# The second MLP's down projection as seven products of quarters, interleaved with the next unit's gate and up products

## The chip, the cores and the metric

The kernel runs on one core of one Trainium2 chip. The metric is device time in microseconds (us). A core has five engines that matter here: TensorE (PE, matrix products), VectorE (DVE), ScalarE (ACT), GpSimd (POOL) and SyncE (SP, which issues most DMAs). Each engine works through its own queue in order and waits on semaphores that other engines and DMAs raise. PE writes its products to PSUM, from which DVE and ACT read them. All data are float32, and 128 is the number of partitions (`P`).

## What is computed

Two layers are run on 2 sequences (`B`) of 1024 tokens (`T`), of 512 features (`D`), together 2048 tokens (`NT`). Each layer adds a product of two branches to its input:

```python
xn = _layernorm(x, axis=-1)
s = _L0_attn_ref(xn, ...)            # delta-rule attention, 16 heads of 128
g = _silu(_L0_ffn_ref(xn, ...))      # ternary MLP, 1408 wide
x = x + s * g
xn = _layernorm(x, axis=-1)
s = _L1_attn_ref(xn, ...)            # gated linear recurrence over the tokens
g = _silu(_L1_ffn_ref(xn, ...))      # the MLP that is changed here
x = x + s * g
```

The second MLP has 4096 hidden features. Its weights come packed as 4-bit codes with one scale for each block of 32:

```python
Wg = dequant_nvfp4(gate_W_packed, gate_scales)      # [4096, 512]
Wu = dequant_nvfp4(up_W_packed, up_scales)          # [4096, 512]
Wd = dequant_nvfp4(down_W_packed, down_scales)      # [512, 4096]
gate = jnp.einsum('th,nh->tn', xt, Wg)
up = jnp.einsum('th,nh->tn', xt, Wu)
gelu = jnp.tanh(0.7978845608028654 * (gate + 0.044715 * gate ** 3)) * gate * 0.5 + gate * 0.5
inter = gelu * up
out = jnp.einsum('tn,hn->th', inter, Wd)
```

The second layer's other branch forms, for each feature, two sigmoid gates by small block-diagonal products, and from them a recurrence h = a h + x over the 1024 tokens.

## The kernel before

**The order of the whole.** `first_layer` runs the attention and the ternary MLP. `Join.run` then goes over the 16 tiles of 128 tokens: `product` (L182) multiplies a tile of the attention's output by its weight (16 matmuls into `jpo`), and `rest` closes the layer for that tile: multiply by the MLP's branch (L199), add the input (L195, and a store of the new x to `x1d`), statistics (L190 to L192), POOL's power, and the normalisation. `turn` then transposes the tile twice (L113): once for the recurrence, copied by ACT and stored to `xd`, and once for the MLP, copied by DVE into quarters of `xq`. After each second tile four DVE subtractions form sums of quarters (t1, t2, t4 and b12). The last tile's `turn` is not called there: it is returned as `late` and called inside `second_layer`.

**Units of the MLP.** `second_layer` splits the 4096 hidden features into 16 groups (`NG`) of 256 and the tokens into the 2 sequences. The loop at the end runs over the groups `g` and, inside, the sequences `b`: one unit is one pair. A unit makes gate [256 x 1024], up [256 x 1024], their product, and the group's share of down, [1024 x 512].

**Gate and up.** Gate and up are matrix products by halves in all three directions, 2 x 2 x 2 blocks, and `four` (L1216 on) makes them by Strassen's scheme in Winograd's form: seven products of quarters in place of eight, with sums of quarters before and after. A `product` (L1229) is two matmuls of 512 columns, contracting 2 x 128 features, into one of four PSUM banks `psa` to `psd`. Banks a, c and d take a second product on top of the first, which adds without another engine. DVE does the other sums (L1239), ACT one copy (L1249), then ACT applies the gelu to the gate's four quarters (L1275), and DVE multiplies with up's quarters (L1281). The results `inter` are four tiles of 128 hidden features x 512 tokens.

**Down.** `down` goes over the unit's 8 tiles of 128 tokens. For each, two matmuls of 512 columns (L1306) contract the group's 2 x 128 hidden features into a bank of the pool `ps_o` (2 buffers), and DVE adds it to `acc`, one [128 x 512] sum for each of the 16 token tiles that stays in SBUF over all groups (L1317; a copy, L1315, in group 0). In the last group each tile is finished at once: SiLU on ACT (L1322), times the recurrence's output `y` on DVE, plus `x1` on POOL or DVE (L1325), and a store issued from ACT's queue.

**Weights.** `group_weights(g + 1)` is called ahead of the group's units. `unpack` loads codes and scales (SP) and turns them into float32 on DVE: five integer operations of 128 x 512, then one multiplication for each destination block (8 of 128 columns each for gate and for up, 2 of 512 for down). `quartered` adds four sums of quarters on POOL for gate and for up. Each of the three weights has two buffers in the pool `wp`; `qp` (2 buffers) holds the codes and scales.

**The recurrence beside.** `recur` handles one quarter of the features (`KC` = 4) of one sequence: block-diagonal products on PE (L1172), sigmoids, tanh and square root on ACT, reciprocals on DVE (L1187), multiplications on POOL (L1188), a scan on DVE, transposes on PE (L1205), a store to `yd`. It is a generator; one step is taken after most of the DVE additions of `four`. Before it, `softplus` (L90, L91 and on) prepares its constants from `vec`, on ACT and DVE.

**What sets the order.** In the second layer, the order on each engine is chosen by the scheduler of the framework from the dependencies and the program's order; nothing is pinned. `first_layer` has a local class `Ordered`, a thin wrapper around an engine that marks its instructions to stay in the order in which they are written while `order["loop"]` is set. Tiles come from pools: a tile takes the buffer of an older one of the same tag, and its first writer waits until that one's users are done. Pools that open after others have closed take over their room in SBUF, with the same kind of waits.

Of the kernel before, what the change touches and what calls it, by code (L numbers as in the profile page):

```python
# [103 lines left out]
def transposed(nc, psp, tag, dst, src, ident, engine, step=1):  # L104
# [11 lines left out]
    if engine == "scalar":  # L116
        nc.scalar.copy(dst, pt)
    else:
        nc.vector.tensor_copy(dst, pt)

# [131 lines left out]
def first_layer(ctx, tc, a, cst, minus_half, keep, xnT, od, gd, then):  # L252
# [247 lines left out]
    class Ordered:  # L500
        def __init__(self, engine):
            self.engine = engine

        def __getattr__(self, name):
            def call(*args, **kw):
                i = getattr(self.engine, name)(*args, **kw)  # L506
                if order["loop"]:
                    tc.keep_in_program_order(i)
                return i

            return call

    PE, DVE, ACT, POOL = (Ordered(e) for e in (nc.tensor, nc.vector, nc.scalar, nc.gpsimd))
# [560 lines left out]
def second_layer(ctx, tc, a, cst, x1d, xd, xq, out, late):  # L1074
# [11 lines left out]

    nc = tc.nc
# [4 lines left out]
    hp = ctx.enter_context(tc.tile_pool(name="l1_h", bufs=2, reuse_waits="tile"))  # L1092
# [4 lines left out]
    ident = cst[:, C_ID, :]  # L1097

# [3 lines left out]
    def unpack(name, src, scales, n, g):  # L1102

        pk = qp.tile([P, n], I32, tag="pk", name=f"pk_{name}_{g}")
        nc.sync.dma_start(pk, src)
        sc = qp.tile([P, n], F32, tag="sc", name=f"sc_{name}_{g}")
        nc.sync.dma_start(sc, scales)
        hi = qp.tile([P, n], I32, tag="hi", name=f"hi_{name}_{g}", bufs=1)
        nc.vector.tensor_scalar(hi, pk, 0xF0, 12, ALU.bitwise_and, ALU.logical_shift_left)
        nc.vector.scalar_tensor_tensor(  # L1110
            pk, in0=pk, scalar=0xF, in1=hi, op0=ALU.bitwise_and, op1=ALU.bitwise_or
        )
        nc.vector.tensor_scalar(hi, pk, 0x00070007, 9, ALU.bitwise_and, ALU.logical_shift_left)
        nc.vector.tensor_scalar(pk, pk, 0x00080008, 12, ALU.bitwise_and, ALU.logical_shift_left)
        nc.vector.tensor_tensor(pk, pk, hi, ALU.bitwise_or)
        halves = pk.bitcast(F16).rearrange("p (n par) -> p par n", par=2)

        def write(dst, par, at=slice(None)):
            nc.vector.scalar_tensor_tensor(
                dst, in0=halves[:, par, at], scalar=16384.0, in1=sc[:, at], op0=ALU.mult, op1=ALU.mult  # L1120
            )

        return write

    def quartered(name, g):

        write = unpack(name, a[name + "pk"][g], a[name + "sc"][g], 512, g)
        w = wp.tile([P, 7, 2, P], F32, tag=f"w_{name}", name=f"w_{name}_{g}")
        for par in range(2):
            for q in range(4):  # L1130
                write(w[:, q, par, :], par, slice(q * P, (q + 1) * P))
# [309 lines left out]
```

## Time and profile before

| | |
|---|---|
| median of 3 runs | 3302.39 us |
| lowest and highest | 3301.01 and 3304.95 us |
| profiled execution, its own time | 3295.65 us |
| its span in the trace | 3293.9 us |
| mean granted TensorE clock | 0.997 of full speed |
| instructions | 36429 |
| DMA traffic | 281.01 MB, 85 GB/s on average |

The page of the profile has the busy time of each engine, the span in 40 equal slices, the DMA queues, the chain of work that ended last, and the costliest groups of instructions. Lines such as "PE 98%" average over stages that differ: up to about 2014 us the first layer runs, with ACT and DVE mostly 30 to 80% busy and DMA at 75 GB/s or more in nearly all slices; behind it the second layer runs, with DMA mostly at 20 to 45 GB/s. PE's row of tenths is 9 or 8 in all slices after the first. One execution's span is 1.75 us shorter than the same execution's time, and that execution lies a little under the lowest of the three timed runs.

### The profile page before, as it was taken

Reading aid. Unit: us, or ns where it says so; the run is one execution under the profiler, and the core shown is the slowest. Engines: PE = TensorE matmul, PEld = TensorE weight load, DVE = VectorE, ACT = ScalarE, POOL = GpSimd, SP = SyncE. Lnnn points to the kernel's source line nnn. Section 1 sums busy time; section 2 is a strip of 40 time slices with the busy share of each in tenths; the row PEclk is TensorE's granted clock in tenths of the full one; section 3 lists DMA queues with packets and bytes.
Section 4 is the critical chain, followed back from the end, with each engine's and each line's share of the span. In section 5 each row is a group of like instructions: output and inputs, shape, how many; then the busy total and the mean of one; then the engine's idle time right before and its main releaser. Section 6 shows DMA issues by size and latency. Waiting matters only on the chain. (4 is left out here: it accounts for less than half of the span.)

```text
span 3293.9 us, 36429 instructions
## 1 busy us (share of the span) xinstructions
PE 3217.0 (98%) x11734; PEld 1807.1 (55%) x11734; DVE 2070.9 (63%) x4398; ACT 1138.5 (35%) x2093; POOL 619.6 (19%) x1008
## 2 busy tenths in 40 slices
PE   7999999999999999998999999999999999999998
PEld 6566756666666666665666444444444444444443
DVE  4566578686878777775664633676666655555545
ACT  3576455555465555444443001222222211100002
POOL 2000022322232222322322200122111100100002
PEclk9999999999999999999999999999999999999999
DMA  5244334444444444434324541111111100000003
GB/s 177 67 140 99 101 108 114 119 133 123 115 113 137 126 125 108 106 107 116 89 76 118 188 151 61 32 32 32 32 32 32 45 26 20 26 20 24 15 0 128
DMA packets 495039, 281.01 MB, mean 85 GB/s; under 512 B 206720, under 2 KB 438912, under 8 KB 494848
## 3 DMA queue, kind: packets, MB, share of 16 engines
q1 hardware_dynamic: 484544, 261.63, 28.2%
q0 software_dynamic: 5696, 8.65, 0.9%
q10 hardware_dynamic: 4608, 8.39, 0.7%
q8 instruction: 94, 1.54, 0.2%
q14 instruction: 97, 0.79, 0.1%
HBM read 179.71 MB, written 86.25 MB: 81 GB/s over the span
## 5 line engine op out<-in xcount | busy, mean ns | idle before, releaser
L1306 PE MATMUL po<-w_d,u 128*128 128x512 f32 x1024 | 455.2, 597 | 11.0 <-DVE acc L1317 5.4
L1306 PEld LDWEIGHTS po<-w_d,u 128*128 128x128 f32 x1024 | 189.3, 190 | 271.2 <-issue 206.1
L506 PE MATMUL pgate<-xnT,wg 128*128 128x512 f32 x512 | 249.4, 597 | 0.0
L1317 DVE TENSOR_TENSOR acc<-acc,po 128x512 f32<-128x512 f32 x240 | 162.9, 682 | 134.0 <-PE po L1306 133.0
L506 PE MATMUL pwv<-xnT,wv 128*128 128x512 f32 x512 | 245.0, 594 | 1.8 <-ACT gate L506 1.8
L506 PE MATMUL pwq<-xnT,wq 128*128 128x512 f32 x512 | 245.1, 593 | 0.0
L1249 ACT COPY g<-pga 128x512 f32<-128x512 f32 x32 | 18.7, 586 | 637.7 <-PE pga L1229 637.7
L506 PE MATMUL pwk<-xnT,wk 128*128 128x512 f32 x512 | 236.8, 593 | 1.6 <-ACT ka L506 1.6
L506 DVE SCALAR_TENSOR_TENSOR v<-prewv,cw,v 128x512 f32<-128x512 f32 x192 | 169.3, 883 | 64.6 <-ACT v L506 53.2
L182 PE MATMUL jpo<-wo,jo 128*128 128x512 f32 x416 | 181.0, 592 | 0.0
L506 DVE SCALAR_TENSOR_TENSOR ka<-prewk,cw,ka 128x512 f32<-128x512 f32 x192 | 146.8, 766 | 36.3 <-ACT ka L506 26.1
L506 DVE SCALAR_TENSOR_TENSOR q<-prewq,cw,q 128x512 f32<-128x512 f32 x192 | 160.3, 835 | 14.4 <-ACT q L506 8.0
L506 DVE TENSOR_TENSOR rr<-rr,zw 128x128 f32<-128x128 f32 x192 | 54.9, 286 | 175.1 <-PE zw L506 173.6
L506 PEld LDWEIGHTS zw<-rr,ground 128*128 128x128 f32 x512 | 96.1, 191 | 125.2 <-issue 98.2
L506 ACT COPY w<-zw 128x128 f32<-128x128 f32 x192 | 50.8, 265 | 328.8 <-PE zw L506 328.6
L1275 ACT ACTIVATE g<-g 128x512 f32<-128x512 f32 x96 | 60.4, 630 | 260.4 <-DVE g L1239 260.2
L506 PEld LDWEIGHTS zw<-w,ground 128*128 128x128 f32 x768 | 111.6, 192 | 66.4 <-issue 55.2
L506 POOL TENSOR_TENSOR rs<-rs,minus_half 128x4 f32<-128x4 f32 x64 | 64.5, 1007 | 421.8 <-DVE rs L506 397.9
L506 POOL TENSOR_TENSOR ot<-ot,gate 128x512 f32<-128x512 f32 x64 | 87.3, 1364 | 298.6 <-ACT ot L506 269.2
L506 ACT ACTIVATE on<-po,nm,rs 128x128 f32<-128x128 f32 x256 | 103.6, 460 | 90.0 <-DVE nm L506 90.0
L506 PEld LDWEIGHTS pwk<-xnT,wk 128*128 128x128 f32 x512 | 90.4, 190 | 76.9 <-issue 72.9
L182 PEld LDWEIGHTS jpo<-wo,jo 128*128 128x128 f32 x416 | 78.0, 190 | 92.3 <-issue 92.3
(248 smaller groups left out, 6520.4 us busy)
## 6 DMA issues: line engine op xcount, KB each, us to landing
e<-gr SPq DMA_DIRECT2D x64, 256.0 KB, 4.0
de<-e SPq DMA_DIRECT2D x64, 256.0 KB, 2.8
dk<-ka SPq DMA_DIRECT2D x32, 512.0 KB, 2.8
kb<-dk SPq DMA_DIRECT2D x64, 256.0 KB, 3.4
eb<-de SPq DMA_DIRECT2D x64, 256.0 KB, 3.0
eg<-egr SPq DMA_DIRECT2D x64, 256.0 KB, 3.9
od<-ot SPq DMA_DIRECT2D x64, 256.0 KB, 2.1
jo<-od SPq DMA_DIRECT2D x16, 1024.0 KB, 6.4
```

The lines of the kernel that those rows point to most:

```text
L182: matmul(po, lhsT=ot[:, h, :], rhs=self.wo[h], start=(h == 0), stop=(h == H - 1))
L506: i = getattr(self.engine, name)(*args, **kw)
L1249: nc.scalar.copy(c21, banks["a"])
L1275: nc.scalar.activation(ge[key], x, AF.Gelu_apprx_tanh)
L1306: nc.tensor.matmul(po, lhsT=inter[par, h][:, i * P : (i + 1) * P], rhs=wd[:, par, :], start=(par == 0), stop=(par == 1),)
L1317: nc.vector.tensor_tensor(dst, dst, po, ALU.add)
```

## The change

**Down by seven products.** For groups 0 to 14, `down` makes the unit's share by the same scheme as gate and up: tokens, hidden features and output features are each halved. Each of the seven products of quarters is made in two steps, one for each half of its 512 tokens. A step (`yield` in `down`) is two matmuls of 256 columns into one bank of `ps_o`, and one DVE addition of 128 x 512 to the accumulator of that product. So `acc` becomes two tiles of seven sums, one set for each sequence, which run over the groups, and the sums after the seven products are made once, by `together`: 28 DVE additions in the last two units. The sums of quarters before are new work in each group: of the weights, four on POOL in `halved`; of the intermediate result, four on POOL in `times`. Group 15 keeps the old form, two matmuls of 512 columns a tile, in `down_last`, which adds to the combined sums.

**Slots.** Down no longer stands behind its own unit. The main loop runs the 14 gate and up products of a unit as 14 slots, and each slot takes one step of the unit before's down, one step of the unpacking for the next group, and, in most slots, one step of the recurrence. The seventh product of up is made in the second slot of the next unit. Group 15's first eight tiles are finished in slots of the last unit, and the other eight behind it.

**Written order.** `Ordered` moves to module level, and the second layer's PE, DVE, ACT and POOL instructions go through it from the start of the main loop: each engine runs them in the order in which they are written. The unpacking of group 0 comes before that.

**Smaller parts.** `four` makes its first, second, fourth and seventh products in bank a (which has two buffers now, and where each of them adds to the one before), the third and sixth in c and the fifth in b; ACT copies bank a out after the first, the second and the fourth. `unpack` is a generator, its last multiplications write several blocks at once (two of 512 columns a weight in place of eight of 128), and its POOL sums run at the end. `recur` runs by halves of 512 tokens, 16 in all, with the state carried over in `carry`, one started in each of 16 units. The last loads of `y` and `x1` use buffers of `qp` and `rp`. The stores of the output are issued from SP's queue, in two halves of a row, and SiLU of a tile is written ahead of the finishing of the tile before.

```diff
...
+class Ordered:
+    def __init__(self, tc, engine, on):
+        self.tc, self.engine, self.on = tc, engine, on
+    def __getattr__(self, name):
+        def call(*args, **kw):
+            i = getattr(self.engine, name)(*args, **kw)
+            if self.on():
+                self.tc.keep_in_program_order(i)
+            return i
+        return call
...
-    hp = ctx.enter_context(tc.tile_pool(name="l1_h", bufs=2, reuse_waits="tile"))
+    hp = ctx.enter_context(tc.tile_pool(name="l1_h", bufs=1, reuse_waits="tile"))
...
+    order = {"on": False}
+    PE, DVE, ACT, POOL = (
+        Ordered(tc, e, lambda: order["on"]) for e in (nc.tensor, nc.vector, nc.scalar, nc.gpsimd)
+    )
...
         halves = pk.bitcast(F16).rearrange("p (n par) -> p par n", par=2)
-        def write(dst, par, at=slice(None)):
-            nc.vector.scalar_tensor_tensor(
-                dst, in0=halves[:, par, at], scalar=16384.0, in1=sc[:, at], op0=ALU.mult, op1=ALU.mult
+        for par in range(2):
+            to = dst(par)
+            k = to.shape[1]
+            DVE.scalar_tensor_tensor(
+                to,
+                in0=halves[:, par, :].rearrange("p (k n) -> p k n", k=k),
+                scalar=16384.0,
+                in1=sc.rearrange("p (k n) -> p k n", k=k),
+                op0=ALU.mult,
+                op1=ALU.mult,
             )
-        return write
+            yield
+        for s in sums:
+            POOL.tensor_tensor(*s)
...
+    def halved(g):
+        w = wp.tile([P, 7, 256], F32, tag="w_d", name=f"w_d_{g}")
+        b11, b12, b21, b22, t1, t2, t4 = (w[:, q] for q in range(7))
+        sums = (
+            (t1, b12, b11, ALU.subtract),
+            (t2, b22, t1, ALU.subtract),
+            (b12, b22, b12, ALU.subtract),
+            (t4, b21, t2, ALU.subtract),
+        )
+        return w, unpack("d", g, lambda par: w[:, 2 * par : 2 * par + 2], sums if g < NG - 1 else ())
...
+    weights, steps = group_weights(0)
+    done(steps)
...
+        def first():
+            product("a", A11, B11, True)
+            ACT.copy(p1, banks["a"])
+        def second():
+            product("a", S2, T2, False)
+            ACT.copy(u1, banks["a"])
+        def third():
+            product("c", S1, T1, True)
+        def fourth():
+            product("a", S3, T3, False)
+            ACT.copy(u2, banks["a"])
+            DVE.tensor_tensor(u2, u2, banks["c"], ALU.add)
+            last((1, 1), u2)
+        def fifth():
+            product("b", A12, B21, True)
+            add(p1, "b", (0, 0))
+        def sixth():
+            product("c", S4, B22, False)
+            add(u1, "c", (0, 1))
+        def seventh():
+            product("a", A22, T4, False)
+            last((1, 0), banks["a"])
+        return first, second, third, fourth, fifth, sixth, seventh
...
+            if key == (0, 1) and g == NG - 1:
+                inters[g, b] = [ups[0, 0], None, ups[0, 1], ups[1, 1]]
+            elif key == (0, 1):
+                s1, s2, s4 = (tile_of(t, u) for t in ("s1", "s2", "s4"))
+                a11, a21, a22 = ups[0, 0], ups[0, 1], ups[1, 1]
+                POOL.tensor_tensor(s1, a21, a22, ALU.add)
+                POOL.tensor_tensor(a21, a11, a21, ALU.subtract)
+                POOL.tensor_tensor(s2, s1, a11, ALU.subtract)
+                inters[g, b] = [a11, None, a21, a22, s1, s2, s4]
+            if key == (1, 0):
+                inters[g, b][A12] = x = ups[key]
+                if g < NG - 1:
+                    POOL.tensor_tensor(inters[g, b][S4], x, inters[g, b][S2], ALU.subtract)
...
+    def down(g, b, wd):
+        left = inters[g, b]
+        for i, j, n in (
+            (A22, T4, 3), (A11, B11, 0), (A12, B21, 1), (S3, T3, 6), (S1, T1, 4), (S2, T2, 5), (S4, B22, 2)
+        ):
+            for half in range(2):
+                po = ps_o.tile([P, 2, 256], F32, tag="pso", name=f"po_{g}_{b}_{n}_{half}")
+                for t in range(2):
+                    c = (2 * half + t) * P
+                    PE.matmul(
+                        po[:, t, :], lhsT=left[i][:, c : c + P], rhs=wd[:, j, :], start=True, stop=True
+                    )
+                dst = acc[b][:, n, half]
+                if g == 0:
+                    DVE.tensor_copy(dst, po)
+                else:
+                    DVE.tensor_tensor(dst, dst, po, ALU.add)
+                yield
...
+    def together(b):
+        P1, P2, P3, P4, P5, P6, P7 = range(7)
+        for dst, x, y in (
+            (P6, P1, P6), (P1, P1, P2), (P7, P6, P7), (P4, P7, P4), (P7, P7, P5), (P5, P6, P5), (P3, P5, P3)
+        ):
+            for half in range(2):
+                DVE.tensor_tensor(acc[b][:, dst, half], acc[b][:, x, half], acc[b][:, y, half], ALU.add)
+                yield
...
-                nc.scalar.activation(dst, dst, AF.Silu)
-                nc.vector.tensor_tensor(dst, dst, y, ALU.mult)
-                last = nc.gpsimd if b == 0 or h or i < 2 else nc.vector
-                last.tensor_tensor(dst, dst, x1, ALU.add)
-                nc.scalar.dma_start(out[ti * P : (ti + 1) * P, :], dst)
...
+    def last_steps(b, h, i, ti, dst):
+        y, x1 = (t.rearrange("p (h n) -> p h n", h=2) for t in at_last.pop(ti))
+        last = POOL if b == 0 or h or i < 2 else DVE
+        return (
+            lambda: DVE.tensor_tensor(dst, dst, y, ALU.mult),
+            lambda: last.tensor_tensor(dst, dst, x1, ALU.add),
+            lambda: nc.sync.dma_start(
+                out[ti * P : (ti + 1) * P, :].rearrange("t (h n) -> t h n", h=2), dst
+            ),
+            load_last,
+        )
...
+                dst = acc[b][:, 3:7:3, i // 2, i % 2] if h else acc[b][:, 0:3:2, i // 2, i % 2]
+                DVE.tensor_tensor(dst, dst, po, ALU.add)
+                ACT.activation(dst, dst, AF.Silu)
+                for step in finishing:
+                    step()
+                finishing = last_steps(b, h, i, ti, dst)
+                yield
+        for step in finishing:
+            step()
+        yield
...
+    order["on"] = True
+    before, recurring, downs, tog = None, none, none, none
+    steps = none
+    for n in range(2 * NG):
+        g, b = n // 2, n % 2
+        if b == 0:
+            wg, wu, wd = weights
+            done(steps)
+            if g < NG - 1:
+                weights, steps = group_weights(g + 1)
+        if n == 2 * NG - 2:
             for _ in range(4):
                 load_last()
-        for b in range(B):
-            inter = up_and_gate(g, b, wg, wu)
-            if g == 0 and b == 0:
-                late(ps_r, "psr", rp.tile([P, KC, P], F32, tag="y", name="xt_last"))
-            down(g, b, wd, inter)
+        if g == NG - 1:
+            tog = together(b)
+        lasts = none
+        if n == 2 * NG - 1:
+            lasts = down_last(0, wd)
+        for f, products in enumerate(up_and_gate(g, b, wg, wu)):
+            for s in range(7):
+                slot = 7 * f + s
+                if s == 1:
+                    if before:
+                        before()
+                else:
+                    products[s - (s > 0)]()
+                if n == 0 and slot == 3:
+                    late(ps_r, "psr", rp.tile([P, KC, P], F32, tag="y", name="xt_last"))
+                next(downs, None)
+                if slot < 10:
+                    next(lasts, None)
+                next(steps, None)
+                if g == NG - 1:
+                    next(tog, None)
+                if slot == 7 and n in starts:
+                    recurring = recur(*starts[n])
+                if slot not in (5, 8, 9):
+                    next(recurring, None)
+            before = products[6]
+        done(downs)
+        downs = down(g, b, wd) if g < NG - 1 else none
+    before()
+    done(tog)
+    done(down_last(1, wd))
```

## The prediction

> **What bounds the kernel now.** I read the page's busy shares, then the second layer's stretch on its own, then TensorE (PE) in order of time, then the waits of PE.
>
> ```profile
> PE 3217.0 (98%) x11734; PEld 1807.1 (55%) x11734; DVE 2070.9 (63%) x4398; ACT 1138.5 (35%) x2093; POOL 619.6 (19%) x1008
> ...
> 2014.47:3284.00 1269.53, 1256.53 (x2954) 548.03 (x2952) 748.22 (x1311) 219.87 (x311) 168.85 (x205) 1.00 0.10 33
> ```
>
> The second line is the stretch from the first gate product to the last down product: stretch, then PE, weight loads, DVE, ACT, POOL. PE is busy for 1256.5 of 1269.5 us, at full clock; DVE has 748 of 1270. Only PE time can pay here.
>
> ```profile
> 2113.01 0.60 PE L1205 MATMUL py<-cst,xc 128*128 128x128 f32 x4
> 2113.44 1.88 PE L1229 MATMUL puc<-xq,w_u 128*128 128x512 f32 x4
> 2115.16 0.60 PE L1205 MATMUL py<-cst,xc 128*128 128x128 f32 x4
> ...
> 2330.12 14.23 PE L1306 MATMUL po<-w_d,u 128*128 128x512 f32 x32
> 2344.19 1.02 PE L1229 MATMUL pga<-xq,w_g 128*128 128x512 f32 x2
> ```
>
> Starts give the true cost, since the shown ends overlap. Four records of 512 columns take 2115.16 - 2113.44 = 1.72 us, 0.4293 us each (one written f32 matmul leaves two records). Four of 128 columns take 2113.44 - 2113.01 = 0.43 us, 0.109 each. A unit's down (32 records) takes 14.07 us, 13.74 of it streaming.
>
> ```profile
> L1306 PE MATMUL po<-w_d,u 128*128 128x512 f32 x1024 | 455.2, 597 | 11.0 <-DVE acc L1317 5.4 <-DVE u L1281 4.0 <-DVE acc L1315 0.8
> L1306 PEld LDWEIGHTS po<-w_d,u 128*128 128x128 f32 x1024 | 189.3, 190 | 271.2 <-issue 206.1
> L1317 DVE TENSOR_TENSOR acc<-acc,po 128x512 f32<-128x512 f32 x240 | 162.9, 682 | 134.0 <-PE po L1306 133.0
> ```
>
> Streaming sum before: gate and up 32 x 56 records, down 32 x 32, the recurrence's pr 64, together 2880 x 0.4293 = 1236.4 us, and 72 records of 128 columns x 0.109 = 7.9: 1244.3. The stretch is 1269.5, so waits and the restarts after them cost **25.2 us**, nearly all PE waiting for DVE (1.2 of it at the first two gate products).
>
> **What the Trainium skill says.** "TensorE: Matmul & The Clock Gate", section "Wait — 56ns, not 53.3ns?", has the start-to-start time as columns / 2.4 GHz plus about 2.5 ns. The trace agrees if an f32 record streams its columns twice: 2 x 512 / 2.4 + 2.5 = 429.2 against 429.3, and 109.2 against 109. The same page, "Step-by-step: what each phase is for", says that PE pulls the next weight load ahead of the running matmul, while ACT and DVE are strict FIFO. The trace agrees on the first: loads of 190 ns cost nothing beside 429 ns, and even 128-column records keep 109 ns. It also says, in "What's actually happening", that an idle window of about 3.4 us halves PE's clock; no wait that long stands in this stretch, so before shows nothing of it.
>
> **The change, part by part.**
>
> 1. Down's products. For 30 of the 32 units, 16 matmuls of 512 columns become 28 of 256. A 256-column record stands in no stream of this trace; on the line through the two measured widths it costs 0.109 + 128 x (0.4293 - 0.109)/384 = 0.216 us. Bounds: 0.2145 (half of 429) and 0.222 (if part of the 190 ns load showed, in proportion as 128-column records with two waits took 0.119). I take 0.216, as 190 < 216. Per unit 32 x 0.4293 = 13.74 becomes 56 x 0.216 = 12.10. Streaming sum after: (1792 + 64 + 64 for the last group, which keeps the old form) x 0.4293 = 824.3, plus 1680 x 0.216 = 362.9, plus 7.9 = 1195.1. **-49.2 us** (ends -51.7 and -39.1).
>
> 2. Waits in the steady loop. A slot is one gate/up product (1.72) and one down step (0.86): 2.58 us. Slots s and s+2 share a bank: "fourth" fills a at slot 4, ACT copies it (586 ns), DVE adds bank c (about 0.69), and "sixth" needs c at slot 6, 5.16 us after slot 4's start. The chain ends at 1.72 + 0.27 + 0.59 + 0.10 + 0.69 = 3.4 us, leaving 1.76 us. A po bank comes back two slots later: its add may start 2.85 us into the slot and must end by 6.88, slack 3.3. DVE's work per unit: 14 evictions x 0.682 (before 8), 6 adds and 4 multiplications (before 10 adds and 4), 24 unpacking steps per two units (about 12 us), the recurrence about 6 us in every second unit: 26 us of a unit's 36, 29 in a unit with a recurrence. The fullest five slots (reciprocals of 1.74 us beside unpacking) put DVE some 1 us late, inside both slacks. ACT gets four more copies (2.3 us), POOL four sums of some 1.4 (the row of 128x512 on POOL has 1.40), due only from slot 6 to 12 of the next unit. So these additions are hidden under PE; uncovered they would cost their own lateness plus the 0.104 us restart seen after each wait. I leave 2 us for the first unit and the last, whose slots have no down step and whose ACT loads tables (1.28 us) eight times.
>
> 3. The seam to the second layer. This is where the change loses.
>
> ```profile
> 2013.52 1.08 PE L113 MATMUL ptr<-cst,jg 128*128 128x128 f32 x8
> 2014.47 1.98 PE L1229 MATMUL pga<-xq,w_g 128*128 128x512 f32 x4
> 2017.33 1.96 PE L1229 MATMUL pgb<-xq,w_g 128*128 128x512 f32 x4 [0.87 <-DVE ln_ve L192]
> ...
> 2013.72 0.69 DVE L199 TENSOR_TENSOR jg<-jpo,jg 128x512 f32<-128x512 f32 x1 [10.29 <-PE jpo L182]
> ...
> 2022.54 0.20 ACT L90 ACTIVATE sp_e<-vec 128x4 f32<-128x4 f32 x1 [5.46 <-DMA vec<-in_vec]
> 2022.76 1.28 ACT L91 ACT_TABLE_LOAD   x1
> ```
>
> The weight pool grows by 2 x 3 KB a partition, so the unpacking buffers move onto the room of an older tile: in the built order the load of group 0's gate codes now waits for the last matmul of the last output product but one (about 1999.1). It lands 2.7 us later (its DMA row). The 21 unpacking steps on DVE, done long before in the old order, now stand ahead of the last tile's L199. From 2002.0: three times (0.43 + 0.69 + 0.42 + 0.42 + 0.69 + 2 x 0.68, and 0.04 between) is about 12.9, plus 0.9 for the layer norm in between: 2015.7 instead of 2013.72. Gate's first product shares that tile's bank and starts at 2016.4. The built order then has the last tile's eight transposes before the second product: multiply, add, copy, statistics, POOL's power (behind four sums of down's weights until 2018.8), normalise: 2020.3. Then ACT: gate's first copy, which frees the accumulating second product, stands behind the softplus constants' Abs and Exp. On SP's queue the constants' load waits behind the x1 store (jx done 2017.1), xc and bd (512 KB): issued 2018.5, landing some 4.4 later as before, 2022.9. Abs 0.2, table 1.28, Exp 0.2, copy 0.6: the second product starts at 2025.2. Without waits it would start at 2014.47 + 1.72 + 0.88 = 2017.1. Wait: **8.2 us**, in place of 1.2. Bounds: 2 if the constants land early and the transposes alone hold it, 12 if the clock halves after it.
>
> So waits go from 25.2 to 8.2 + 2 = 10.2: **-15.0 us**.
>
> 4. The tail.
>
> ```profile
> 3287.32 1.15 ACT L1322 ACTIVATE acc<-acc 128x512 f32<-128x512 f32 x2 [3.57 <-POOL acc L1325]
> ...
> 3289.19 1.29 DVE L1325 TENSOR_TENSOR acc<-acc,x 128x512 f32<-128x512 f32 x2
> ```
>
> The stores leave ACT's queue for SP's, so the last SiLUs no longer wait behind a store that waits for POOL. From PE's end: 0.27, add 0.69, multiply and add of the tile before 1.2, multiply 0.7, add 0.7, then 3.4 from the last add to the end as before: 7.0 instead of 3293.9 - 3284.0 = 9.9. **-2.9 us** (bounds 0 and -3.5; half-size descriptors in the stores may take some back).
>
> 5. Hidden: the first layer's PE order is the same; its DVE loses the early unpacking, with room to spare (idle 10 us of each 14.6 there). The adding up of the seven accumulators (28 adds of 0.69) stands one to a slot in the last two units.
>
> **Sum** -49.2 - 15.0 - 2.9 = -67.1 us on the profiled span of 3293.9 (3295.65 with what lies around it): 3228.6. The runs' median, 3302.39, lies 6.7 higher and I carry that over: **3235 us**.
>
> **Rivals.**
> - A: the written order keeps as many waits as the old one (24 us besides the seam), as DVE and ACT run in fixed order and one late head holds all behind it. For it: PE's waits today are of this kind. Against: the slacks above. 24 instead of 2: 3257 us.
> - B: the seam costs next to nothing, since loads land earlier than I chain them: 3235 - 7 = 3228. Against: four separate queues have to be early.
> - C, slower: the handover of bank c from slot 4 to slot 6 (and 11 to 13). It decides from a DVE lateness of 1.76 + 67/30 = 4.0 us at one such slot in every unit. If DVE stood two slots (5.2 us) late, PE would lose 3.4 us a unit, 102 in all: 3235 + 102 = 3337. For it: evictions rise from 8 to 14 and DVE is in written order. Against: 26 us of work in 36.
>
> **Chances.** Forecast 0.62, A 0.22, B 0.10, C 0.05, and 0.01 for an end between A and C near no change. The range takes forecast, A and B with the open ends of parts 1 and 3: 3221 to 3261. This kernel's measurement tells 0.2% (6.6 us) from no change. Faster 0.94, same 0.01, slower 0.05.
>
> **What would show it.** 1680 records of 256 columns starting 0.216 us apart beside 190 ns loads; the second gate product some 8 us late, after a copy behind Exp; slots of 2.58 us with PE's waits under 3 us from the second unit on; under 7.5 us from the last matmul to the end. It is wrong if 256-column starts exceed 0.222, or if PE's list of waits names DVE or ACT in every unit.

## The result, and the profile after

The kernel after takes **3248.24 us** (median of 4 runs, 3247.51 to 3250.49), the kernel before 3303.43 us (4 runs, 3301.01 to 3304.95): a ratio of 0.9835, with a 95% interval from 0.9818 to 0.9852, so 55 us or 1.65% less. The forecast was 3235 us, with a range of 3221 to 3261: the direction and the range held, but the likeliest value was 13 us too low. The profiled execution took 3248.6 us, its span is 3246.8 us.

From the page after, the busy line, DVE's additions of down, and the two PE groups that carry its products (columns: engine, operation, out<-in, shapes and count | busy us, mean ns | idle us before, and what ended it):

```profile
PE 3169.7 (98%) x12454; PEld 1958.8 (60%) x12454; DVE 2142.2 (66%) x4286; ACT 1245.7 (38%) x2259; POOL 824.1 (25%) x1204
...
L130 DVE TENSOR_TENSOR acc<-acc,po 128x512 f32<-128x512 f32 x408 | 278.2, 682 | 219.9 <-PE po L130 218.8
...
L130 PE MATMUL po<-w_d,i 128*128 128x256 f32 (+1 forms) x1024 | 275.4, 392 | 0.8 <-DVE i L130 0.8
...
L130 PE MATMUL po<-w_d,s 128*128 128x256 f32 x720 | 184.8, 379 | 0.0
```

L130 is the line of the helper that marks the order, so groups are told apart by their tiles. In the old kernel PE waited 11.0 us inside down; now the groups of down wait 0.8 us. The shown durations (379 ns) overlap; the start times give the cost. PE in order of time, in a stretch of the first units:

```profile
2103.82 1.03 PE L130 MATMUL po<-w_d,i 128*128 128x256 f32 x4
2104.69 1.88 PE L130 MATMUL pgc<-xq,w_g 128*128 128x512 f32 x4
...
2107.27 1.88 PE L130 MATMUL pga<-xq,w_g 128*128 128x512 f32 x4
```

A step of down, four records of 256 columns, takes 2104.69 - 2103.82 = 0.87 us, 0.216 us a record, and a slot 2107.27 - 2104.69 = 2.58 us. Both are the predicted numbers.

Then the largest waits of PE from the last transposes of the first layer on (waited for: us in total, times, longest):

```profile
PE pga L130 <- ACT g L130: 4.5, 1, 4.5
PE pga L130 <- DVE jg L215: 4.1, 1, 4.1
PE pgc L130 <- DVE g L130: 3.0, 10, 0.3
```

These are the idle times that the profile shows. Start-to-start spacing also has the slow restart after each wait (0.104 us in each of the ten on bank c) and the records that ran at half clock; I use it from here on, and count every excess over 0.4293, 0.216 and 0.109 us a record. For the stretch from the end of the first layer's last transposes to PE's last matmul:

| us | before | after |
|---|---|---|
| whole stretch | 1269.57 | 1215.13 |
| lost at the seam (first 40 us) | 1.48 | 13.78 |
| lost later | 24.14 | 6.80 |
| from the last matmul to the end | 9.89 | 9.61 |
| end of the first layer | 2014.42 | 2022.09 |

So streaming fell by 54.44 - (25.62 - 20.58) = 49.4 us, waits by only 5.0, the tail by 0.3: together 54.7, beside 55.2 between the medians. The last row is taken up in the first experiment: the changed kernel reached the same point of the same PE work 7.7 us later in its profiled run.

**The seam.** The PE, ACT, DVE and POOL rows around it:

```profile
2021.19 1.08 PE L113 MATMUL ptr<-cst,jg 128*128 128x128 f32 x8
2026.39 3.68 PE L130 MATMUL pga<-xq,w_g 128*128 128x512 f32 x4 [4.13 <-DVE jg L215]
2031.12 1.13 PE L113 MATMUL ptr<-cst,xn_last 128*128 128x128 f32 x8 [1.04 <-DVE xn_last L219]
2036.74 3.62 PE L130 MATMUL pga<-xq,w_g 128*128 128x512 f32 x4 [4.49 <-ACT g L130]
...
2034.40 0.20 ACT L90 ACTIVATE sp_e<-vec 128x4 f32<-128x4 f32 x1 [2.01 <-DMA vec<-in_vec]
2034.63 1.28 ACT L91 ACT_TABLE_LOAD   x1
...
2036.03 0.57 ACT L130 COPY g<-pga 128x512 f32<-128x512 f32 x1
...
2012.40 0.69 DVE L130 TENSOR_TENSOR pk_g<-pk_g,hi_g 128x512 int32<-128x512 int32 x1
...
2014.34 0.42 DVE L130 TENSOR_SCALAR hi_u<-pk_u 128x512 int32<-128x512 int32 x1
...
2014.55 3.65 POOL L130 TENSOR_TENSOR w_g<-w_g 128x256 f32<-128x256 f32 x4 [3.10 <-issue]
...
2015.92 0.83 DVE L130 TENSOR_SCALAR hi_u<-pk_u 128x512 int32<-128x512 int32 x1
...
2017.65 1.10 DVE L130 TENSOR_TENSOR pk_u<-pk_u,hi_u 128x512 int32<-128x512 int32 x1
...
2025.66 0.68 DVE L215 TENSOR_TENSOR jg<-jpo,jg 128x512 f32<-128x512 f32 x1
```

Every link of the predicted chain is there: group 0's unpacking stands on DVE ahead of L215 of the last tile, the transposes come ahead of the second gate product, and that waits for a copy behind Abs, table load and Exp. Two things are new. The four records of a gate product took 3.6 us in place of 1.88, both times after an idle time of more than 4 us: half clock (the trace grants 0.50 from 2026.46 and again from 2033.29 us). And DVE's integer steps stretched from 0.69 and 0.42 us to 1.10 and 0.83 while POOL was making its sums.

**The loop.** One of the ten waits on bank c, PE first, then DVE, then POOL:

```profile
2151.16 1.98 PE L130 MATMUL pgc<-xq,w_g 128*128 128x512 f32 x4 [0.30 <-DVE g L130]
...
2143.73 1.59 DVE L130 SCALAR_TENSOR_TENSOR w_u<-pk_u,sc_u 128x512 f32<-128x512 f16 x1
2145.25 0.81 DVE L130 TENSOR_SCALAR ga<-ga 128x256 f32<-128x256 f32 x1
...
2149.70 0.81 DVE L130 TENSOR_SCALAR ga<-ga 128x256 f32<-128x256 f32 x1
2150.44 0.68 DVE L130 TENSOR_TENSOR g<-g,pgc 128x512 f32<-128x512 f32 x1
...
2143.51 1.26 POOL L130 TENSOR_TENSOR s<-i,s 128x512 f32<-128x512 f32 x1
2144.73 1.17 POOL L130 TENSOR_TENSOR gx<-gx,mu 128x256 f32<-128x256 f32 x1
```

The sixth product needs bank c back from the addition at 2150.44, which DVE reached late. The multiplication into w_u took 1.59 us where the same form takes 0.68 when POOL is idle. The ga step took 0.81; between 2050 and 3200 us, the six such steps that met no POOL instruction took 0.28 each, the other 58 took 0.28 to 1.36. The loss is 0.57 us a time, with the restart.

**The tail.** DVE, then SP's queue:

```profile
3237.82 0.68 DVE L130 TENSOR_TENSOR acc<-acc,po 128x512 f32<-128x512 f32 x1
3239.83 0.69 DVE L130 TENSOR_TENSOR acc<-acc,lgx 128x512 f32<-128x512 f32 x1 [1.34 <-DMA lgx<-yd]
...
3241.74 0.69 DVE L130 TENSOR_TENSOR acc<-acc,lga 128x512 f32<-128x512 f32 x1 [0.49 <-DMA lga<-yd]
...
3233.58 0.55 SPq L1399 DMA_DIRECT2D out<-acc  x1
3234.22 0.56 SPq L1389 DMA_DIRECT2D lgx<-yd  x1
...
3235.47 0.55 SPq L1399 DMA_DIRECT2D out<-acc  x1
3236.12 0.56 SPq L1389 DMA_DIRECT2D lga<-yd  x1
```

The last loads of y and x1 stand on SP's queue behind stores, and the stores wait for additions, most of them on POOL. The SiLUs no longer wait; DVE waits for these loads instead.

### The profile page after: what moved, and what is told of

Its sections match the earlier page's. It is cut to its first block, busy times and chain, and to the rows that moved or that the text cites. A ratio compares the mean times of both kernels' runs of the same rounds, so it can differ in the third digit from the quotient of the medians.

```text
span 3246.8 us, 38192 instructions
## 1 busy us (share of the span) xinstructions
PE 3169.7 (98%) x12454; PEld 1958.8 (60%) x12454; DVE 2142.2 (66%) x4286; ACT 1245.7 (38%) x2259; POOL 824.1 (25%) x1204
## 5 line engine op out<-in xcount | busy, mean ns | idle before, releaser
L130 DVE TENSOR_TENSOR acc<-acc,po 128x512 f32<-128x512 f32 x408 | 278.2, 682 | 219.9 <-PE po L130 218.8
L130 PEld LDWEIGHTS po<-w_d,i 128*128 128x128 f32 x1024 | 194.5, 190 | 143.6 <-issue 113.3
L130 PE MATMUL po<-w_d,i 128*128 128x256 f32 (+1 forms) x1024 | 275.4, 392 | 0.8 <-DVE i L130 0.8
L130 PE MATMUL pga<-xq,w_g 128*128 128x512 f32 x512 | 244.2, 600 | 8.6 <-ACT g L130 4.5
L130 PE MATMUL pgate<-xnT,wg 128*128 128x512 f32 x512 | 248.6, 595 | 0.0
L130 PE MATMUL pwv<-xnT,wv 128*128 128x512 f32 x512 | 245.0, 594 | 1.8 <-ACT gate L130 1.8
L130 PE MATMUL pwq<-xnT,wq 128*128 128x512 f32 x512 | 245.2, 594 | 0.0
L130 PE MATMUL pwk<-xnT,wk 128*128 128x512 f32 x512 | 240.2, 600 | 2.3 <-ACT ka L130 2.3
L130 PE MATMUL pua<-xq,w_u 128*128 128x512 f32 x512 | 240.7, 592 | 0.0
L130 ACT COPY g<-pga 128x512 f32<-128x512 f32 x96 | 56.2, 585 | 442.4 <-PE pga L130 435.2
L130 DVE SCALAR_TENSOR_TENSOR v<-prewv,cw,v 128x512 f32<-128x512 f32 x192 | 169.5, 884 | 65.1 <-ACT v L130 53.1
L130 PEld LDWEIGHTS po<-w_d,s 128*128 128x128 f32 x720 | 136.8, 190 | 95.4 <-issue 85.1
L130 PE MATMUL po<-w_d,s 128*128 128x256 f32 x720 | 184.8, 379 | 0.0
L130 ACT COPY w<-zw 128x128 f32<-128x128 f32 x192 | 50.6, 264 | 340.4 <-PE zw L130 340.1
L130 POOL TENSOR_TENSOR rs<-rs,minus_half 128x4 f32<-128x4 f32 x64 | 64.4, 1007 | 427.6 <-DVE rs L130 397.5
L130 PEld LDWEIGHTS zw<-rr,ground 128*128 128x128 f32 x512 | 97.1, 193 | 125.2 <-issue 98.5
L130 DVE SCALAR_TENSOR_TENSOR ka<-prewk,cw,ka 128x512 f32<-128x512 f32 x192 | 148.1, 773 | 36.1 <-ACT ka L130 26.8
L130 DVE TENSOR_TENSOR rr<-rr,zw 128x128 f32<-128x128 f32 x192 | 54.8, 285 | 176.3 <-PE zw L130 174.8
L130 DVE SCALAR_TENSOR_TENSOR q<-prewq,cw,q 128x512 f32<-128x512 f32 x192 | 160.0, 833 | 14.4 <-ACT q L130 7.9
L130 POOL TENSOR_TENSOR ot<-ot,gate 128x512 f32<-128x512 f32 x64 | 86.7, 1355 | 300.2 <-ACT ot L130 270.8
```

## The experiments

**Theory**: nearly the whole gain (49.4 of 54.7 us) is the streaming; of the waits, the seam keeps 13.8 us (unpacking ahead of the last layer norm, constants ahead of a copy), the loop 6.8 us because DVE stretches beside POOL, and the tail moved its wait to SP's queue. **Rivals**: the gain is in slots and order; the loop's waits come from too many DVE instructions; the changed kernel slows its first layer.

**1. The kernel before, once more** (no edit).

> The kernel before, profiled once more. Theory S (the 7.7 us by which the changed kernel reaches the end of the first layer later, 2021.2 against 2013.5 us, are scatter between executions: the instructions of PE there are the same): the last transposes of the first layer start near 2021 us, span near 3301, and the second layer's stretch is again 1269 to 1271 us. Rival (the changed kernel really slows its first layer): they start again near 2013.5 us and the span is near 3294.

It took 3299.8 us. Its first layer ended at 2018.55 us, 4.1 later than in the profile shown of before; the second layer's stretch is again 1269.57 us, the tail 9.88. So the second layer repeats to 0.01 us and the first layer scatters, by more than half of the 7.7 us. The runs with the changed second layer put its end anywhere from 2014.6 to 2022.1, and 11 runs of the kernel before in the same session ran from 3296.28 to 3303.43 us. PE's 8782 records up to that point have the same tiles in the same order in both kernels. The 7.7 us are mostly or wholly scatter: the profile shown of before was one of the short executions. What goes with the scatter is PE's time at half clock: from 30 us to the first layer's end it is 13.7 us in the profile shown of before, 27.3 in the second one and 34.1 in the changed kernel's. Over all 14 profiles the end comes later the longer this time is (correlation 0.94); that it causes the delay is not shown by an experiment. From here on I compare stretches, not spans.

**2. The old down in slots.** Slots and written order stay; the products and their sums go:

```diff
-        return w, unpack("d", g, lambda par: w[:, 2 * par : 2 * par + 2], sums if g < NG - 1 else ())
+        return w, unpack("d", g, lambda par: w[:, 2 * par : 2 * par + 2], ())
...
-                POOL.tensor_tensor(s1, a21, a22, ALU.add)
...
-                        po[:, t, :], lhsT=left[i][:, c : c + P], rhs=wd[:, j, :], start=True, stop=True
+                        lhsT=left[2 * h + par][:, i * P : (i + 1) * P],
+                        rhs=wd[:, 2 * par : 2 * par + 2, :],
...
-            tog = together(b)
+            tog = none
```

> The changed kernel with the old down (two matmuls of 512 columns for each of 8 tiles, no sums of quarters) in the first eight slots of the next unit, slots and written order kept. Streaming theory (the gain is the 1/8 fewer columns; slots and order give only the waits): 49 us of streaming come back, some of the 5.7 us of waits on bank c go, as DVE and POOL have less to do: 3248 + 49 - 4 = 3293, within 4. Rival (the gain comes from the slots and the written order, and the products of quarters cost as much as they save): 3255 or less.

Measured 3291.22 us (ratio to before 0.9970, 0.9959 to 0.9981), stretch 1261.55: 46.4 us more than after. The loss behind the seam is 3.75 us, against 6.80. That is the streaming theory's number. Slots, written order and the smaller parts, without the products, bring 9 us of the 55.

**3. The products without the written order.**

```diff
-    order["on"] = True
```

> The changed kernel without the written order: the scheduler orders PE, DVE, ACT and POOL in the second layer. Streaming theory: the same records stream, and only waits differ: 3248 to 3275, the upper end if the scheduler's order brings back the 24 us of waits of the kernel before. Rival (the written order is what the gain rests on): 3290 or more.

Measured 3278.23 us (0.9934, 0.9919 to 0.9949), stretch 1250.02: 34.9 us more than after, 3 us over the theory's upper end and 12 under the rival's. The waits from the end of the first layer on are

```profile
PE pgc L130 <- DVE g L130: 17.3, 15, 1.3
PE po L130 <- DVE acc L130: 13.1, 21, 1.0
PE pga L130 <- DVE jg L215: 5.0, 1, 5.0
```

as the largest, or 40.5 us behind the seam with restarts, more than the 24.1 of the kernel before. So both theories were short: the same 3672 records stream in any order, and with them the 49 us are saved, but in the scheduler's order the products also bring more waits, on bank c and on the banks of down, and the written order takes these away. Neither part alone gives the sum of the two.

**4. Without POOL's sums of the intermediate result.**

```diff
-                s1, s2, s4 = (tile_of(t, u) for t in ("s1", "s2", "s4"))
...
-                POOL.tensor_tensor(s1, a21, a22, ALU.add)
-                POOL.tensor_tensor(a21, a11, a21, ALU.subtract)
-                POOL.tensor_tensor(s2, s1, a11, ALU.subtract)
-                inters[g, b] = [a11, None, a21, a22, s1, s2, s4]
+                inters[g, b] = [a11, None, a21, a22, *still]
...
-                    POOL.tensor_tensor(inters[g, b][S4], x, inters[g, b][S2], ALU.subtract)
```

> Leaves out the four sums of quarters of the intermediate result on POOL in each unit of groups 0 to 14 (down multiplies still tiles of zeros in their place), so that DVE has the same list of instructions. Theory P (DVE falls behind bank c because its SBUF to SBUF instructions stretch beside POOL's): DVE's multiplications into w_u go from 1.5 and 1.0 us towards 0.68, its additions into pk_u from 1.45 to 0.68, and the ten waits of PE on bank c (0.57 us each) fall to three or fewer. Rival N (too many DVE instructions in these slots, whatever POOL does): the ten waits stay at 0.4 us or more each.

The kernel leaves the sums out, so its output is not the layer's; what counts is the time of the same DVE instructions. All ten waits on bank c went; behind the seam 1.09 us are left of 6.80. PE's list of waits names POOL in neither kernel, so it was not the sums themselves that PE waited for. DVE's groups between 2050 and 3200 us, in the changed kernel:

```profile
L130 DVE SCALAR_TENSOR_TENSOR w_u<-pk_u,sc_u 128x512 f32<-128x512 f16 x30 | 38.1, 1270 | 0.0
L130 DVE TENSOR_TENSOR pk_u<-pk_u,hi_u 128x512 int32<-128x512 int32 x15 | 20.9, 1395 | 0.0
L130 DVE RECIPROCAL ga<-ga 128x256 f32<-128x256 f32 x32 | 56.1, 1753 | 1.1
```

and without these sums:

```profile
L130 DVE SCALAR_TENSOR_TENSOR w_u<-pk_u,sc_u 128x512 f32<-128x512 f16 x30 | 23.5, 783 | 0.0
L130 DVE TENSOR_TENSOR pk_u<-pk_u,hi_u 128x512 int32<-128x512 int32 x15 | 10.3, 684 | 0.0
L130 DVE RECIPROCAL ga<-ga 128x256 f32<-128x256 f32 x32 | 56.1, 1753 | 1.1
```

The same instructions of DVE take half the time (the additions into pk_u) and three fifths of it (the multiplications into w_u, ten of which still met POOL's other work); theory P holds. The reciprocals, and the additions that read PSUM (682 ns in both), don't change. In the changed kernel 16 of the 32 reciprocals and 138 of the 396 additions ran beside a POOL instruction, and took no longer than the rest. The Trainium skill, "SBUF — State Buffer", section "Who interferes with whom", gives a reason: DVE and GpSimd share a pair of SBUF ports as an exclusive lock, so a DVE instruction with two SBUF inputs, or a `tensor_scalar` in its two-port mode, can be held up by a GpSimd instruction that reads SBUF; one with at most one SBUF input in its plain mode is not. These rows, and the ga steps above, agree. The multiplication into w_u, a form that the section doesn't name, has two SBUF inputs and behaves by its rule.

**5. Where the recurrence starts.**

```diff
-    starts = {1 + i * 27 // 15: h for i, h in enumerate(halves)}
+    starts = dict(zip([*range(1, 28, 2), 28, 29], halves))
```

> The changed kernel with 14 of the 16 recurrence halves started in odd units (1, 3, to 27) and the last two in 28 and 29; before, ten started in even units, and each of the ten waits on bank c lies in the unit after one of these. Theory P (there the recurrence's and u's unpacking instructions on DVE meet POOL's sums): at most two waits on bank c are left and PE's waits behind the seam fall from 6.8 to 2.5 us or less. Rival (any unit with a recurrence beside it loses as much): ten or more such waits, in other units, 5 us or more.

Two waits on bank c are left, both behind the last two starts, and the loss behind the seam is 2.73 us, slightly over the 2.5 expected; 3240.80 us (0.9817, 0.9803 to 0.9832). It is a cure that leaves nothing out. It also corrects the picture: here DVE's instructions beside POOL are as long as before (1395 ns into pk_u, 1224 into w_u), and yet only two waits are left. So the stretching alone does not hold PE; it takes the recurrence's DVE steps in the same slots. Between too long and too many instructions this run does not decide; experiment 4 does.

**6. The seam, one cause at a time.** First the order of two pools, which decides whose old room group 0's codes load into:

```diff
-    wp = ctx.enter_context(tc.tile_pool(name="l1_w", bufs=2, side="right", reuse_waits="tile"))
     qp = ctx.enter_context(tc.tile_pool(name="l1_q", bufs=2, side="right", reuse_waits="tile"))
+    wp = ctx.enter_context(tc.tile_pool(name="l1_w", bufs=2, side="right", reuse_waits="tile"))
```

> The changed kernel with the pool of codes and scales opened ahead of the pool of weights, so that group 0's codes no longer load into the room of the last output products; most of its unpacking then stands ahead of tile 13's layer norm. Theory U (group 0's unpacking on DVE in front of tile 15's layer norm delays the first gate product): the wait of 4.3 us in front of the first gate product goes to under 1 us and takes the 1.4 us of halved clock behind it along, the second gate product still waits for the softplus constants: 4 to 6 us less in all. Rival (the constants' chain decides alone, since the second product can't start before it): 0 to 1 us less.

3240.23 us (0.9819, 0.9802 to 0.9835). The first gate product starts right behind the transposes (by 0.05 us), and the stretch is 4.8 us shorter (1210.29): theory U. The layer norm and the constants then show what they had hidden:

```profile
2019.27 1.98 PE L130 MATMUL pga<-xq,w_g 128*128 128x512 f32 x4
2023.95 1.13 PE L113 MATMUL ptr<-cst,xn_last 128*128 128x128 f32 x8 [2.70 <-DVE xn_last L219]
2028.10 3.75 PE L130 MATMUL pga<-xq,w_g 128*128 128x512 f32 x4 [3.01 <-ACT g L130]
```

Then the softplus constants, in the first unit instead of ahead of it:

```diff
-    softplus(nc, cp, spa, vec[:, 0, :], 1.0, ("e", "w", "w2"))
...
+                if n == 0 and slot == 10:
+                    softplus(both, cp, spa, vec[:, 0, :], 1.0, ("e", "w", "w2"))
```

> The changed kernel with the softplus constants made in slot 10 of the first unit in place of ahead of the main loop. Theory V (ACT's copy of the first gate product stands behind Abs and Exp, which wait for the constants' load): the first gate product still waits 4.3 us, the second starts right behind the eight transposes, and 4.5 to 6 us go. Rival (DVE's or POOL's part of the last tile holds the second product): under 1.5 us less.

The median, 3240.71 us (0.9820, 0.9805 to 0.9834), looks like theory V, but the stretch says otherwise: 1214.01, only 1.1 us shorter, and the profiled first layer ended at 2017.1. The second product does start right behind the transposes. But PE's clock, halved at the first idle time, stayed so until 2031.8 (10.2 us), 5.2 us of idle time at the first product were untouched, and in slot 10 up's product on bank c now waited 1.7 us for DVE, which stood in the softplus chain. This expectation missed: the time is on the rival's side, though not for the rival's reason.

Both edits:

> Both edits: pool of codes ahead of the weights', softplus constants in slot 10. Theory U and V: the waits from the first layer's last transposes to the third gate product fall from 13.8 us to 3 or less, no record runs at half clock there, and the time is 9 to 12.5 us under the changed kernel, about 3236 where that has 3247. Rival (one delay hides behind the other or the moved unpacking is late elsewhere): 6 us or less.

3234.89 us (0.9802, 0.9788 to 0.9817); stretch 1207.54, 7.6 us shorter, between the two expectations. No record ran at half clock, but the 2.8 us wait for the last layer norm remains, and slot 10's wait. That pointed at the third cause: the transposes of the last tile, which only the second unit needs, stand ahead of the second gate product because the scheduler places them. The third edit writes them into slot 5, in order, and makes the constants before the first layer's last loop of products, where ACT and DVE have room:

```diff
-                if n == 0 and slot == 3:
+                if n == 0 and slot == 5:
+                    late.func.__self__.tc = types.SimpleNamespace(
+                        nc=types.SimpleNamespace(tensor=PE, vector=DVE, scalar=ACT, sync=nc.sync)
+                    )
                     late(ps_r, "psr", rp.tile([P, KC, P], F32, tag="y", name="xt_last"))
...
+    softplus(nc, eo, spa, vec[:, 0, :], 1.0, ("e", "w", "w2"))
+    m4 = eo.tile([P, KC], F32, name="m4")
+    nc.vector.tensor_scalar(m4, spa, 4.0, None, ALU.mult)
     late = joining.run(xd, xq, eo)
```

> The pool of codes ahead of the weights', the softplus constants made ahead of the last product loop of the first layer, and the last tile's transposes written into slot 5 of the first unit, in order. Theory: with all three causes gone, the waits of PE from the first layer's last transposes on fall from 13.8 us (6.2 with two of them, the second one by another edit) to 3 or less, no record runs at half clock, and the second layer's stretch is 1204 to 1206 us, against 1215.1. Rival (the last tile's layer norm holds the gate products whatever is moved): 1207 or more.

3231.99 us (0.9792, 0.9776 to 0.9809); stretch 1204.73, loss at the seam 3.41 us, slightly over the 3 expected, no half clock:

```profile
2017.25 1.98 PE L131 MATMUL pga<-xq,w_g 128*128 128x512 f32 x4 [2.02 <-DVE jg L216]
2020.11 1.96 PE L131 MATMUL pga<-xq,w_g 128*128 128x512 f32 x4 [0.88 <-DVE ln_ve L209]
```

**7. The stores on ACT's queue.**

```diff
-            lambda: nc.sync.dma_start(
+            lambda: nc.scalar.dma_start(
                 out[ti * P : (ti + 1) * P, :].rearrange("t (h n) -> t h n", h=2), dst
```

> The changed kernel with the output's stores issued from ACT's queue again, all else kept. Theory T (the tail kept its length because the last loads of y stand on SP's queue behind stores that wait for POOL): DVE's waits of 1.3 and 0.5 us for those loads go and the time from PE's last matmul to the end falls from 9.6 to 7.8 us, within 0.5. Rival (it was ACT's queue that set the old tail, and the SiLUs wait behind the stores again): 9.3 us or more.

The tail fell from 9.61 to 8.40 us and DVE's two waits for loads are gone, as theory T has it, if a little less than expected: the last SiLU now starts 1.4 us behind the addition that it needs, after a store on ACT's queue that waits for POOL. But the time is 3249.05 us (0.9840, 0.9825 to 0.9855), nothing gained, as the stretch grew from 1215.13 to 1218.50. In the last unit, where the first eight tiles are finished in slots, ACT now stood behind stores that waited for POOL, and PE behind ACT. The waits of PE from 2050 us on, then ACT there:

```profile
PE pua L130 <- ACT i L130: 3.1, 2, 1.8
...
3212.55 0.54 ACTq L1399 DMA_DIRECT2D out<-acc  x1
3213.12 1.28 ACT L130 ACT_TABLE_LOAD   x1 [2.05 <-POOL acc L130]
```

**8. Together.** Seam, starts and stores:

> All together: seam3, odd_starts and stores_act. If the three are separate, the stretch is 1215.1 - 10.5 - 5 = 1199.6 us and the tail 7.8: some 17 us under the changed kernel, 3230 us where that has 3247, within the 4 us by which the first layer scatters. If one brings no more than another's leftovers, 3236 or more.

3235.49 us (0.9799, 0.9785 to 0.9814), stretch 1204.42, tail 8.46: the waits of the last unit, 3.6 us, ate what the starts brought, so the parts were not separate. With ACT's queue for the last eight tiles alone:

```diff
-            lambda: nc.scalar.dma_start(
+            lambda: (nc.scalar if b else nc.sync).dma_start(
```

> As best2, but only the last eight tiles' stores go through ACT's queue; the first eight, made in slots of the last unit, stay on SP's. Theory: the two waits of 1.6 and 2.0 us of PE on ACT's copies in the last unit, which stood with ACT behind stores that wait for POOL, are gone (stretch 1200.5 to 1201.5 us, against 1204.4), and the tail keeps 8.4 us: 15 us less than the changed kernel from the first layer's end on, about 3232 us. Rival (the copies were late for another reason, the unpacking or the recurrence moved to unit 29): the waits on ACT stay, stretch 1204 or more.

**3228.92 us** (median of 5 runs, 3223.64 to 3231.04; 0.9776, 0.9763 to 0.9790), stretch 1200.80, tail 8.46. This beats both kernels: from the first layer's end on, 15.5 us less than the changed one. What PE still waits for is the list below, 6.2 us with restarts:

```profile
PE pga L131 <- DVE jg L216: 2.0, 1, 2.0
PE pgc L131 <- DVE g L131: 1.2, 2, 0.8
PE pga L131 <- DVE ln_ve L209: 0.9, 1, 0.9
PE po L131 <- DVE i L131: 0.8, 1, 0.8
```

## Why the prediction was right, and where its terms were off

- **Part 1, products of down.** Right: 0.216 us a record in the median of 1680, -49.4 us measured where -49.2 stood. The 190 ns weight loads stayed hidden beside 216 ns.
- **Part 2, waits in the loop.** Mis-sized: 2 us stood for it, 6.80 were measured. DVE's total was right (842 us busy in the 1211 us from the first gate product on, 25 us a unit, where 26 stood), but the step "put DVE some 1 us late, inside both slacks" took its durations from rows where POOL was idle. Beside POOL, whose busy time in the second layer the change itself raises from 169 to 383 us, they grew to twice as long and more, and ten slots ran through their slack. Experiments 4 and 5 show it. The trace of before had the sign: there a multiplication at L1281, 0.69 us long when POOL is idle, took up to 2.30 beside it. It is the place that rival C named, with a price of 0.57 us in ten units in place of 3.4 us in thirty.
- **Part 3, the seam.** Mechanism right, size wrong: 13.8 us measured, 8.2 forecast, over the bound of 12. The unpacking, summed at 12.9 us, was longer by some 2.3, for the same reason as in part 2, so the first product came 4.3 us late where 1.9 stood. With that the x1 store, which stands ahead of the constants' load on SP's queue, was 2.9 us later than in the forecast's chain, and the load took 5.3 us in place of 4.4: the second product started 14.65 us after the transposes' end, where 10.8 stood. The other 1.7 us are records at half clock behind it; the forecast had the halved clock in its upper end only.
- **Part 4, the tail.** Wrong in its outcome: -0.3 us in place of -2.9. The sum ran along DVE and left out SP's queue, where the loads of y for the last tiles stand behind the stores that the change had just put there; these loads held DVE for 1.8 us. That is not all: with the stores on ACT's queue (experiment 7) the tail is 8.4 us, 1.4 over the 7.0 forecast, as the last SiLU then waits behind a store. Neither queue gives the chain that was summed.
- **Part 5, hidden work.** Held: PE waits for none of the combining additions, and its order in the first layer is the same.
- **From span to median.** The 6.7 us carried over were scatter of the first layer, and the second profile of before (3299.8 us) shows part of it. To carry them was right: the profiled run after (3248.6 us) lies at its median.

The three mis-sized terms, 5.6 + 4.8 + 2.6, come to the 13 us by which the forecast was low. All three erred to the same side, so no luck of opposite errors kept the time within the range; but two of the signs named for the forecast, waits under 3 us and a tail under 7.5, did not come. Rival A, that the written order keeps the old waits (24 us), is refuted by the 6.80 us of the table, and experiment 3 shows that it is the scheduler's order that has them. Rival B is out by the seam's 13.8 us.

## What to carry to other kernels

When work is added on GpSimd, price the VectorE instructions beside it again: here one with two SBUF inputs went from 0.68 to as much as 1.59 us, and a short `tensor_scalar` from 0.28 to as much as 1.36. A saving in streamed columns arrives in full only if the order keeps the extra handovers off the tensor engine: here products in the scheduler's order gave 22 us, slots and written order with the old products 9, both together 55. And when a DMA changes its queue, look at what already stands on that queue, and at what its wait will hold up.

## What the runs showed of the hardware

- PE at half clock takes 0.853 us for a record of 512 columns in place of 0.429. No single length of idle time decides. In the run with the pool exchange alone (experiment 6) the clock kept full speed behind the idle time of 2.70 us, and was halved at 2026.62, half way into the next one of 3.01; in the first layer of the first run of experiment 8, 2.23 us were enough. PE ran at half clock in the first layer of the kernel before as well, from 345.5, 1499.2 and 1509.5 us on; the prediction had looked at the second layer alone. The Trainium skill, "TensorE: Matmul & The Clock Gate", section "What's actually happening", tells of a free-running window of 3413 ns, and the traces agree: within each of the 14, all changes of the granted clock behind the first 30 us lie on one grid of 3.413 us.
- How busy PE was in a window of that grid tells what follows. All 104 changes to half clock, up to 3200 us, came behind a window in which PE's shown records cover at most 54%; none of the others at full clock, some 12,750, was covered below 43%. All 104 changes back came behind a window of 83% or more, while 28 windows of 80% or less kept the clock at half. The shown ends of matmuls are modelled, so the shares are rough. In the pool exchange the two windows up to 2026.62 were covered to 43 and 33%: by these shares neither wait alone would have halved the clock, which is worked out and was not run.
- The first layer, with the same instructions on PE, ended between 2014.4 and 2022.1 us over the profiled executions, while the second layer of the kernel before repeated to 0.01 us in its two profiles. Differences of medians below some 5 us say little here; the stretch behind the first layer tells a tenth of a us.
